# A convolution-attention kernel: the queues of all five engines ordered by a table of places, and the softmax's divisors kept in PSUM

## The chip, the cores and the metric

The kernel runs on one core of one Trainium2 chip. The metric is the device time of one execution in microseconds (us), and less is better. The core has a matrix engine (TensorE, in the profile PE, with its weight loads shown apart as PEld), a vector engine (VectorE, DVE), a scalar engine (ScalarE, ACT), a general one (GpSimd, POOL) and SyncE (SP), which here only issues DMAs. Each of the five works through a queue of its own, in order, and waits for the others by semaphores.

## The reference, cut to what matters

The input is 16 images of 56 x 56 pixels with 384 channels. Layer 0 is a group norm, then attention over a 3 x 3 neighbourhood with three dilations (one for each third of the channels, four heads of 32 channels in each), then a projection, added to the input. Layer 1 is a group norm and a depthwise 3 x 3 convolution with signs as weights, added again.

```python
def _dilate_attention(q, k, v, head_dim, kernel, dil):
    ...
    attn = jnp.einsum('bgdn,bgdkn->bgnk', qg, ku) * scale     # 9 neighbours
    attn = jax.nn.softmax(attn, axis=-1)
    out = jnp.einsum('bgnk,bgdkn->bgnd', attn, vu)
...
qkv = jnp.einsum('bchw,oc->bohw', xc, w_qkv)
outs = [_dilate_attention(qkv[:, 0, i], qkv[:, 1, i], qkv[:, 2, i], hd, 3, (1, 2, 3)[i]) for i in range(3)]
y = jnp.stack(outs, axis=3).reshape(b, h, w, c)
return jnp.einsum('bhwc,oc->bhwo', y, w_proj) + b_proj
...
x = x + _L0_conv_ref(_gn(x), w_qkv, w_proj, b_proj)
x = x + _L1_conv_ref(_gn(x), w)                               # depthwise, weights sign(clip(w))
```

## The kernel before

An image is cut into 7 chunks of 8 rows (448 pixels), so there are 112 chunks. Data lie with the channels on the partitions, 128 channels to a group, three groups. Everything is float32 but the attention weights, which are split into three bfloat16 terms. All loops are unrolled in Python, and three plans lay out a chunk's work:

- `plan_a`: a chunk of x is loaded, transposed on PE (`turn`, tile `pt_x`), copied out by ACT (`xa`), its statistics taken by DVE, and stored channel by channel.
- `plan_b`, attention. `normalise` (ACT, tile `xn`); `k_or_v` (PE, tile `pkv`, then a copy on ACT and two small DMAs for the rows shared with the next chunk) and `query` (PE, tile `pq`) for each of three groups. `score`, nine times: DVE multiplies a query by three shifted keys (`t`). `score_rounds`: PE sums these over a head's channels in bursts (`ps`, from 32-column pieces of the array). The softmax in five pieces: a copy `sT` on ACT, its transposes `pt_s` on PE, maximum and difference on DVE, `exp` on ACT, sum, reciprocal and product on DVE (L556 to L558, the divisors `sm` in SBUF), a cast on ACT and three operations on POOL that make the three terms; then a transposing DMA. `weigh`, nine times: PE spreads three weights over a head's channels (`pb_a`, three bfloat16 matmuls of 24 rows), DVE multiplies them by shifted values (`w`, L600), and POOL adds (L608, L611, L612) until `y` is there. `out_project`, three times: PE (`po`), then DVE adds the residual and takes statistics, and the sum is stored.
- `plan_c`, convolution: for two channel groups PE takes the side taps (`pc`, 32-column pieces), ACT normalises their input (`z`) and makes a term `u`, DVE adds three operands. For the third group ACT makes nine products (`taps_g`, L818) and POOL adds them (L825 to L834). Then everything is transposed back (`turn`, tile `pt_o`), copied out by ACT and stored.
- `group_norm`, once for each image and layer, turns statistics into a scale and a shift, in six pieces over PE, DVE and POOL.

A stage is one chunk in the steady part: the tile `sT` is written once in each. A stage is nine slices (`STEP`). Every piece is put down with `at(slice, order, piece)`: the slice is counted from the chunk's own start `t0`, and the second number orders the pieces within one slice (SOFTMAX first, LOADS last). At the end all pieces are traced in that order. The framework's scheduler then makes the five queues out of what was traced; it goes by priority in the order of tracing, by its own estimate of when operands are ready, and by when a buffer comes free. So an engine's queue may differ from the traced order, and a group of matmuls may be divided. `in_one_go` gives the later matmuls of a group a high priority and keeps them in order. Chunk m's attention starts at slice 9m; its stage A runs up to 12 stages ahead, its convolution ten stages behind.

Buffers that matter below: PSUM has 8 banks: three for everything that is short (`ps_mt`: `pt_x`, `pkv`, `po`, `pt_s`, `pc`, `pt_o` and the norm's tiles), one for `pq`, one for `ps`, three for one `pb_a`. In SBUF there are four `t`, four `w`, two `z`, two `x1`, two `xg`, two `xa`, one `u`, one `xin`, one `xr`.

Of the kernel before, what the change touches and what calls it, by code (L numbers as in the profile page):

```python
# [31 lines left out]
TERMS = 3  # L32


@with_exitstack
def dilated_attention_then_binary_conv(
# [263 lines left out]
    def in_one_go(matmuls):  # L300

        matmuls[0]()
        with tc.high_priority():
            for m in matmuls[1:]:
                tc.keep_in_program_order(m())

    def group_norm(sets):

        had = {}
        L = len(sets)

        def channels(n, j):
            if "ch" not in had:
                had["ch"] = st_p.tile([P, L, NG, 2], F32, tag=f"ch{L}", name="ch")
            nc.vector.bn_aggr(had["ch"][:, n, j, :], sets[n][0][:, j].rearrange("p c s -> p (c s)"))  # L320

        def mean():
            had["pair"] = pair = st_p.tile([GN_G, L, 3], F32, tag=f"pair{L}", name="pair")
            pm = ps_mt.tile([P, 512], F32, tag="mt", name="pm")
            for j in range(NG):
                nc.tensor.matmul(
                    pm[:GN_G, 0:L], gsel[:, j], had["ch"][:, :, j, 0], start=(j == 0), stop=(j == NG - 1)
                )
            nc.vector.tensor_scalar_mul(pair[:, :, 2], pm[:GN_G, 0:L], -1.0 / GN_CH)

        def deviation():

            ch = had["ch"]
            pb = ps_mt.tile([P, 512], F32, tag="mt", name="pb")
            for j in range(NG):
                nc.tensor.matmul(
                    pb[:, j * L : (j + 1) * L], gselT[:, j], had["pair"][:, :, 2], start=True, stop=True
                )
            had["dev"] = dev = st_p.tile([P, L, NG], F32, tag=f"dev{L}", name="dev")
            nc.vector.tensor_tensor(  # L340
                dev, pb[:, : NG * L].rearrange("p (j l) -> p l j", l=L), ch[:, :, :, 0], ALU.add
            )
            nc.gpsimd.tensor_tensor(dev, dev, dev, ALU.mult)
            nc.gpsimd.tensor_tensor(dev, dev, ch[:, :, :, 1], ALU.add)

        def variance():
            dev = had["dev"]
            pv = ps_mt.tile([P, 512], F32, tag="mt", name="pv")
            for j in range(NG):
                nc.tensor.matmul(pv[:GN_G, 0:L], gsel[:, j], dev[:, :, j], start=(j == 0), stop=(j == NG - 1))  # L350
            had["var"] = var = st_p.tile([GN_G, 3, L], F32, tag=f"var{L}", name="var")
            v, r = var[:, 0], var[:, 1]
            nc.vector.tensor_scalar(v, pv[:GN_G, 0:L], 1.0 / GN_CH, 1e-5, op0=ALU.mult, op1=ALU.add)

            ri = r.bitcast(I32)
            nc.vector.tensor_single_scalar(ri, v.bitcast(I32), 1, op=ALU.arith_shift_right)
            nc.vector.tensor_scalar(ri, ri, -1, RSQRT_BITS, op0=ALU.mult, op1=ALU.add)

        def invert():

            var, pair = had["var"], had["pair"]
            v, r, t = var[:, 0], var[:, 1], var[:, 2]
            for step in range(3):
                nc.gpsimd.tensor_tensor(t, r, r, ALU.mult)
                nc.gpsimd.tensor_tensor(t, t, v, ALU.mult)
                nc.gpsimd.tensor_scalar(t, t, -0.5, 1.5, op0=ALU.mult, op1=ALU.add)
                nc.gpsimd.tensor_tensor(pair[:, :, 1] if step == 2 else r, r, t, ALU.mult)
            nc.gpsimd.tensor_tensor(pair[:, :, 0], pair[:, :, 2], pair[:, :, 1], ALU.mult)

        def spread_out():  # L370
            pair = had["pair"]
            pp = ps_mt.tile([P, 512], F32, tag="mt", name="pp")
            for j in range(NG):
                nc.tensor.matmul(
                    pp[:, 2 * L * j : 2 * L * (j + 1)], gselT[:, j], pair[:, :, 0:2], start=True, stop=True
                )
            mr = st_p.tile([P, NG, L, 2], F32, tag=f"mr{L}", name="mr", bufs=5 - L)
            nc.vector.tensor_copy(mr.rearrange("p j l s -> p (j l s)"), pp[:, : 2 * L * NG])
            for n, (_, done, for_convolution) in enumerate(sets):
                if not for_convolution:  # L380
                    done(mr[:, :, n])
                    continue

                pz = ps_mt.tile([P, 512], F32, tag="mt", name="pz")
                for s in range(JG * NQ):
                    of_set = gselT[:, s // NQ, s % NQ * HD : s % NQ * HD + HD]
                    for ky in range(3):
                        nc.tensor.matmul(
                            pz[ky * HD : (ky + 1) * HD, 2 * s : 2 * s + 2], of_set, pair[:, n, 0:2],
                            start=True, stop=True,  # L390
                        )
                mrz = st_p.tile([K3, JG, NQ, 2], F32, tag="mrz", name="mrz")
                nc.vector.tensor_copy(mrz.rearrange("p j q s -> p (j q s)"), pz[:K3, : 2 * JG * NQ])
                done(mr[:, :, n], mrz)

        return channels, mean, deviation, variance, invert, spread_out
# [4 lines left out]
    pieces = {}  # L401

    def at(when, order, piece):

        pieces.setdefault((when, order), []).append(piece)
# [8 lines left out]
    def plan_a(m, t0):  # L414
# [17 lines left out]
        def turn(j):  # L432
# [5 lines left out]
            if b == 0:  # L438

                if j == 0:  # L440
                    pool, tag = ((xn_p, "xn"), (xn_p, "xn"), (xn_p, "xn"), (xr_p, "xr"), (t_p, "t"), (w_p, "w"),
                                 (w_p, "w"))[c]
                    first[c] = pool.tile([P, NG, PX], F32, tag=tag, name="x_first")
                xa = first[c][:, j]
            else:
                xa = xa_p.tile([P, PX], F32, tag="xa", name="xa")
            nc.scalar.copy(xa, pt[:, :PX])  # L447
            nc.vector.bn_stats(stats0[b][:, j, c, :], xa)
            if b:
                nc.sync.dma_start(xd[b][j * P : (j + 1) * P, c * PX : (c + 1) * PX], xa)  # L450
            elif j == NG - 1:
                nc.scalar.dma_start(chunk_of(xd[b], c), first[c])

        at(t0 - 3 if b else FIRST + 2 * max(c - 2, 0), LOADS, load)
        for j in range(NG):
            at(t0 + 2 * j if b else FIRST + 2 * c + 1, STAGE_A, lambda j=j: turn(j))

    def plan_b(m, t0):
# [21 lines left out]
        def k_or_v(g, which):  # L480
# [4 lines left out]
            project(pk, (1 + which) * C + g * P)  # L485
            nc.scalar.copy(cur[:, d : d + ROWS, d : d + W], rows(pk[:, :PX]))  # L486
            if c == 0:
# [7 lines left out]
        def query(g):  # L495
            had["q"] = pq = ps_q.tile([P, 512], F32, tag="q", name="pq")
            project(pq, g * P)
# [23 lines left out]
        def score(i):  # L521

            g, ky = divmod(i, 3)
            d = DIL[g]
            qg = rows(had["q"][:, :PX])
# [15 lines left out]
        def softmax_1():  # L541

            sT = s_p.tile([P, NSUB * NPAD * HEADS], F32, tag="sT", name="sT")[:, :PX]
            nc.scalar.copy(sT, had.pop("ps")[:, :PX])
            pt = ps_mt.tile([P, 512], F32, tag="mt", name="pt_s")
            for s in range(NSUB):
                nc.tensor.transpose(pt[:SUB, s * P : (s + 1) * P], sT[:, s * SUB : (s + 1) * SUB], permf)
            pt4 = pt[:SUB].rearrange("p (s v) -> p s v", s=NSUB)[:, :, :NR]
            mx = s_p.tile([SUB, NSUB, GH], F32, tag="mx", name="mx")
            nc.vector.reduce_max(mx, by_neighbour(pt4).rearrange("p s o k -> p s k o"), axis=AX.X)  # L550
            nc.vector.tensor_tensor(by_neighbour(weights), by_neighbour(pt4), over_neighbours(mx), ALU.subtract)
            nc.scalar.activation(weights, weights, AF.Exp, scale=SCALE)

        def softmax_2():
            sm = s_p.tile([SUB, NSUB, GH], F32, tag="mx", name="sm")
            nc.vector.reduce_sum(sm, by_neighbour(weights).rearrange("p s o k -> p s k o"), axis=AX.X)  # L556
            nc.vector.reciprocal(sm, sm)
            nc.vector.tensor_tensor(by_neighbour(weights), by_neighbour(weights), over_neighbours(sm), ALU.mult)  # L558

        EIGHTS = "p (u k) -> p u k"  # L560
        e8 = ew.rearrange(EIGHTS, k=8)
        term = [e3.rearrange("p s u (r k) -> p (s u r) k", r=4)[:, :, 8 * t : 8 * t + 8] for t in range(TERMS)]

        def softmax_3():

            nc.scalar.copy(term[0], e8)  # L566

        def softmax_4():
            had["rest"] = rest = s_p.tile([P, NSUB * NPAD * HEADS], F32, tag="sT", name="rest")[:SUB]
            nc.gpsimd.tensor_tensor(rest.rearrange(EIGHTS, k=8), e8, term[0], ALU.subtract)  # L570

        def softmax_5():
            r8 = had["rest"].rearrange(EIGHTS, k=8)
            nc.gpsimd.tensor_copy(term[1], r8)
            last_term[m] = nc.gpsimd.tensor_tensor(term[2], r8, term[1], ALU.subtract)

# [392 lines left out]
```

## Time and profile before

| what | value |
|---|---|
| time of three runs | 5153.74 us median (5148.28 to 5155.06) |
| the profiled execution's own time | 5160.07 us |
| its span, first to last instruction | 5157.9 us |
| mean granted PE clock | 0.979 |
| POOL `w<-w` (L608) | 672 of 3050 ns |
| DVE `w<-pb_a,v` (L600) / `t<-pq,k` (L529) | 1008 of 1549 ns / 1008 of 1547 ns |
| ACT `z` (L721) / `m<-zg,ktap` (L818) | 840 of 752 ns / 945 of 659 ns |
| DVE `ew<-ew,sm` (L558) | 112 of 1055 ns |
| loads `x<-x1d` / `z<-x1d` / `xin` | 5.7 / 3.8 / 7.8 us from issue to landing |

The profile is of one execution of its own. Busy shares are means over the whole span, and a busy PE is not PE at its peak, since its matmuls overlap; the distance from one matmul's start to the next is the better measure. float32 matmuls are two instructions each in the trace, so `pkv x12` is two projections and `pq x6` is one.

### The profile page before, as it was taken

What the parts mean: (1) busy time and instruction counts of PE and PEld (TensorE: products, weight loads), DVE (VectorE), ACT (ScalarE), POOL (GpSimd) and SP (SyncE); (2) the same over time, 40 slices, a digit from 0 to 9 for tenths busy, and PEclk for the clock granted to TensorE, in tenths of its full rate; (3) what the DMA queues carried; (4) which work ended last, traced back from release to release, by engine and by line L of the source; (5) the groups of instructions that cost most, each with busy time, mean ns of one, the idle gap of its engine ahead of it and who ended that gap; (6) DMA issues with size and microseconds to landing.
All of it is one profiled execution on the core that took longest, in us unless ns stands there. A gap on an engine that the chain in (4) does not pass through costs nothing. (4 is left out here: it accounts for less than half of the span.)

```text
span 5157.9 us, 72661 instructions
## 1 busy us (share of the span) xinstructions
PE 4967.5 (96%) x25093; PEld 2259.1 (44%) x25093; DVE 4475.9 (87%) x4575; ACT 2478.8 (48%) x4365; POOL 4248.0 (82%) x2998
## 2 busy tenths in 40 slices
PE   7999999999999999999999999999999999999975
PEld 4444444444444444444444444444444444444422
DVE  4888888888898888898888898888889988888876
ACT  3223545555454555545545554554555545444445
POOL 2778888888888888889888888888889888888891
PEclk8999999999999999999999999999999999999986
DMA  6443666666566665666666666666656656555455
GB/s 194 125 123 112 171 170 175 171 168 172 166 172 167 169 169 167 172 163 172 170 175 169 168 174 169 168 168 167 173 164 174 168 166 170 146 135 139 119 144 162
DMA packets 813957, 836.45 MB, mean 162 GB/s; under 512 B 362643, under 2 KB 782870, under 8 KB 813590
## 3 DMA queue, kind: packets, MB, share of 16 engines
q1 hardware_dynamic: 805606, 819.81, 57.8%
q10 hardware_dynamic: 7984, 12.00, 0.7%
q8 instruction: 199, 3.26, 0.3%
q14 instruction: 168, 1.38, 0.1%
HBM read 477.43 MB, written 231.21 MB: 137 GB/s over the span
## 5 line engine op out<-in xcount | busy, mean ns | idle before, releaser
L608 POOL TENSOR_TENSOR w<-w 128x1344 f32<-128x1344 f32 x672 | 2049.5, 3050 | 300.8 <-DVE w L600 262.3
L600 DVE TENSOR_TENSOR w<-pb_a,v 128x1344 f32<-128x1344 f32 x1008 | 1561.6, 1549 | 132.5 <-PE pb_a L593 102.1
L529 DVE TENSOR_TENSOR t<-pq,k 128x1344 f32<-128x1344 f32 x1008 | 1527.6, 1547 | 130.0 <-PE pq L476 128.8
L476 PE MATMUL pkv<-xn,wqkvT 128*128 128x448 f32 x3924 | 1553.3, 545 | 26.7 <-ACT xa L447 26.2
L476 PEld LDWEIGHTS pkv<-xn,wqkvT 128*128 128x128 f32 x3924 | 727.6, 191 | 706.4 <-issue 631.6
L476 PE MATMUL pq<-xn,wqkvT 128*128 128x448 f32 x1962 | 862.4, 567 | 0.0
L626 PE MATMUL po<-y,wprojT 128*128 128x448 f32 x2016 | 836.2, 551 | 20.1 <-POOL y L612 17.3
L721 ACT ACTIVATE z<-z,mrz 96x448 f32<-96x448 f32 x840 | 580.4, 752 | 262.6 <-DMA z<-x1d 220.6
L825 POOL TENSOR_TENSOR m<-m 128x1344 f32<-128x1344 f32 x210 | 640.0, 3047 | 68.6 <-ACT m L818 62.6
L514 PE MATMUL ps<-t,sel 128*32 128x448 f32 x6048 | 661.1, 546 | 1.8 <-DVE t L529 1.7
L818 ACT ACTIVATE m<-zg,ktap 128x448 f32<-128x448 f32 x945 | 568.9, 659 | 17.6 <-POOL m L825 8.5
L626 PEld LDWEIGHTS po<-y,wprojT 128*128 128x128 f32 x2016 | 375.8, 191 | 378.8 <-issue 346.2
L486 ACT COPY v<-pkv 128x448 f32<-128x448 f32 x336 | 178.5, 531 | 755.2 <-PE pkv L476 755.1
L476 PEld LDWEIGHTS pq<-xn,wqkvT 128*128 128x128 f32 x1962 | 339.4, 190 | 349.9 <-issue 349.9
L593 PE MATMUL pb_a<-aT,spread 24*128 24x448 bf16 x3024 | 370.4, 360 | 52.6 <-DVE w L600 48.4
L629 DVE SCALAR_TENSOR_TENSOR xr<-po,bias,xr 128x448 f32<-128x448 f32 x336 | 227.5, 677 | 210.7 <-PE po L626 205.8
L612 POOL TENSOR_TENSOR y<-y,w 128x448 f32<-128x448 f32 x336 | 381.7, 1136 | 20.3
L611 POOL TENSOR_TENSOR y<-w 128x448 f32<-128x448 f32 x336 | 382.3, 1138 | 17.3
L447 ACT COPY xa<-pt_x 128x448 f32<-128x448 f32 x315 | 167.4, 533 | 474.6 <-PE pt_x L435 469.2
L593 PEld LDWEIGHTS <-spread 24*128 24x128 bf16 x3024 | 102.5, 91 | 627.5 <-issue 608.6
L570 POOL TENSOR_TENSOR rest<-ew,e 112x512 f32<-112x512 f32 x112 | 130.2, 1163 | 292.5 <-ACT e L566 291.3
L752 PE MATMUL pc<-z,kdiag 96*32 96x440 f32 x3360 | 359.5, 546 | 8.8 <-POOL z L723 7.6
(141 smaller groups left out, 4745.8 us busy)
## 6 DMA issues: line engine op xcount, KB each, us to landing
z<-x1d SPq DMA_DIRECT2D x570, 224.0 KB, 3.8
xr<-xd SPq DMA_DIRECT2D x112, 672.0 KB, 4.3
x1d<-xr SPq DMA_DIRECT2D x112, 672.0 KB, 3.2
xn<-xd SPq DMA_DIRECT2D x109, 672.0 KB, 4.6
xin<-in_x_dram SPq DMA_DIRECT2D x105, 672.0 KB, 7.8
xd<-xa SPq DMA_DIRECT2D x315, 224.0 KB, 3.6
out_dram<-osb SPq DMA_DIRECT2D x420, 168.0 KB, 3.5
x<-x1d SPq DMA_DIRECT2D x80, 560.0 KB, 5.7
```

The lines of the kernel that those rows point to most:

```text
L476: nc.tensor.matmul(dst[:, :PX], wqkvT[:, cc, o0 : o0 + P], had["xn"][:, cc, :], start=(cc == 0), stop=(cc == NG - 1))
L514: return nc.tensor.matmul(had["ps"][32 * j : 32 * j + 32, :PX], sel[:, s0 : s0 + 32], tk, start=(issued[j] == 1), stop=(issued[j] == len(r ...
L529: nc.vector.tensor_tensor(t.rearrange("p k (r w) -> p k r w", w=W), q3, k3, ALU.mult)
L593: return nc.tensor.matmul(pb[:, kx, :PX].rearrange("p (s n) -> p s n", s=NSUB), spread[rows_of, v % 2, :], had["a"][rows_of, :, v // 8, :] ...
L600: nc.vector.tensor_tensor(w.rearrange("p k (r w) -> p k r w", w=W), pb[:, :, :PX].rearrange("p k (r w) -> p k r w", w=W), three(kv[1][g][m ...
L608: nc.gpsimd.tensor_tensor(w0, w0, w, ALU.add)
L611: nc.gpsimd.tensor_tensor(y, w0[:, 0], w0[:, 1], ALU.add)
L612: nc.gpsimd.tensor_tensor(y, y, w0[:, 2], ALU.add)
L626: nc.tensor.matmul(po[:, :PX], wprojT[:, g, j * P : (j + 1) * P], had[f"y{g}"], start=(g == 0), stop=(g == NG - 1))
L721: nc.scalar.activation(z, z, AF.Identity, bias=mrz[:, j, q, 0:1], scale=mrz[:, j, q, 1:2])
L818: nc.scalar.activation(rows(t[:, kx]), zp[:, ky : ky + ROWS, kx : kx + W], AF.Copy, scale=ktap[:, JG, o : o + 1])
L825: nc.gpsimd.tensor_tensor(had["m"], had["m"], t, ALU.add)
```

## The change

Three things change. The tables of slices go, and a table `WHEN` takes their place: it holds, for each kind of work and each of its repetitions, one number for every engine's part of it, in slices from t0. The pieces become generators that `yield` between the parts of different engines, and `put` places each part by its own number. While the place lies from 0 to 9 x 112 + 14 = 1022, every instruction of the five queues is tied to the one traced before it on its engine (`pin`), so that each queue has exactly the traced order; outside that stretch the scheduler orders as before. And the divisors `sm` are written to a PSUM tile in the bank of `ps`, not to SBUF.

```diff
+WHEN = dict(
+    load_in=[[1.86]],
+    turn_in=[[6.026, 7.853, 8.103, 9.616], [8.887, 8.898, 11.431, 13.527], [9.427, 9.669, 9.841, 12.978]],
+    load_x=[[-16.698]],
+    normalise=[[-14.8], [-11.887], [-14.8]],
+    k=[[-7.795, -7.784, -7.773], [-6.349, -6.338, -2.8], [-3.845, -3.158, -1.177]],
+    v=[[7.341, 7.352, 8.827], [5.08, 6.207, 9.429], [7.847, 8.378, 9.967]],
+    query=[[4.619], [7.271], [8.939]],
+    score=[[4.825], [5.138], [5.149], [7.626], [7.637], [7.877], [10.723], [10.734], [10.745]],
+    burst=[[5.75], [8.056], [11.108]],
+    softmax=[[11.283, 12.017, 12.028, 12.151, 13.101, 13.445, 14.191, 14.202, 14.629, 15.664]],
+    weigh=[[17.248, 17.838, 20.379], [18.267, 18.278, 20.39], [20.023, 20.034, 20.421], [20.194, 20.223,
+        23.104], [20.709, 20.932, 24.835], [21.886, 22.889, 25.743], [23.429, 23.44, 25.754], [23.902, 25.371,
+        27.079], [25.884, 25.895, 27.807]],
+    load_residual=[[28.002]],
+    out_project=[[28.362, 28.749, 29.829, 108.842], [28.647, 29.405, 34.465, 55.401], [30.355, 30.533, 31.612,
+        34.476]],
+    load_g=[[9.822]],
+    normalise_g=[[10.839]],
+    taps=[[11.121, 12.433], [11.132, 12.731], [11.143, 14.144]],
+    sums=[[18.53], [18.541], [18.813]],
+    load_x1=[[5.837]],
+    load_z=[[-1.661, 3.083], [1.74, 3.075]],
+    normalise_z=[[5.379, 5.39], [7.123, 7.821]],
+    column=[[6.427], [7.222]],
+    convolve=[[5.632, 6.438], [8.054, 8.065]],
+    turn_out=[[19.405, 19.416, 19.866], [20.439, 20.499, 20.51], [21.786, 21.835, 27.008], [22.192, 22.518,
+        22.582]],
+    statistics=[[33.116, 34.74, 35.945, 35.956, 37.004, 37.015, 37.026, 37.993, 38.004, 39.539, 40.578, 40.589,
+        40.926, 40.937, 41.368]],
+)
...
-        with tc.high_priority():
+        with nullcontext() if newest.get("pinned") else tc.high_priority():
             for m in matmuls[1:]:
-                tc.keep_in_program_order(m())
+                if newest.get("pinned"):
+                    m()
+                else:
+                    tc.keep_in_program_order(m())
...
+    def put(t0, what, piece):
+
+        places = WHEN[what]
+        for n, stages in enumerate(places):
+            of_it = (n,) if len(places) > 1 else ()
+            if len(stages) == 1:
+                at(t0 + stages[0], lambda of_it=of_it: piece(*of_it))
+                continue
+            steps = piece(*of_it)
+            for when in stages:
+                at(t0 + when, lambda steps=steps: next(steps, None))
...
-            sm = s_p.tile([SUB, NSUB, GH], F32, tag="mx", name="sm")
+            yield
+            sm = ps_s.tile([P, 512], F32, tag="s", name="psm")[:SUB, : NSUB * GH]
+            sm = sm.rearrange("p (s k) -> p s k", s=NSUB)
             nc.vector.reduce_sum(sm, by_neighbour(weights).rearrange("p s o k -> p s k o"), axis=AX.X)
             nc.vector.reciprocal(sm, sm)
+            yield
             nc.vector.tensor_tensor(by_neighbour(weights), by_neighbour(weights), over_neighbours(sm), ALU.mult)
...
-        at(t0 - 18, LOADS, load_x)
...
-        at(t0 + 9, SOFTMAX, softmax_1)
-        at(t0 + 10, SOFTMAX, softmax_2)
...
-            at(t0 + 14 + i - (pair == 1), WEIGH_AHEAD if pair == 0 else WEIGH, lambda i=i: weigh(i))
-        at(t0 + 20, LOADS, load_residual)
-        for j in range(NG):
-            at(t0 + 24 + j, PROJECT, lambda j=j: out_project(j))
+        put(t0, "load_x", load_x)
...
+        put(t0, "softmax", softmax)
+        put(t0, "weigh", weigh)
...
+            t0 += max(0, WHEN["statistics"][0][-1] + 1.1 - 36)
...
-            ahead = 8 if c else 1
+            ahead = 8 if c > 1 else 1
...
+    def pin(engines):
+
+        traced = nc.cur_bb.bb.instructions
+        new = []
+        for ins in reversed(traced):
+            if ins is newest.get("seen"):
+                break
+            new.append(ins)
+        newest["seen"] = traced[-1]
+        for ins in reversed(new):
+            if ins.engine not in FIXED:
+                continue
+            prev = newest.get(ins.engine)
+            newest[ins.engine] = ins
+            if prev is not None and ins.engine in engines:
+                tc.add_manual_dep(
+                    ins, prev.name,
+                    mybir.DependencyInfo(mybir.DependencyClass.NoSync, mybir.DependencyReason.DATA),
+                    reason="stage order",
+                )
+
+    for when in sorted(pieces):
+        newest["pinned"] = FROM <= when < UNTIL
+        for piece in pieces[when]:
             piece()
+            pin(FIXED if newest["pinned"] else ())
```

The numbers of one list are the parts of one piece in order: for a softmax ACT, PE, DVE, ACT, DVE (sum and reciprocal), DVE (product), ACT, POOL, POOL, SP; for `weigh` PE, DVE, POOL; for `out_project` PE, DVE, DVE, SP; for `turn_in` PE, ACT, DVE, SP; for `k` and `v` PE, ACT, SP; for `convolve` PE, DVE; for `turn_out` PE, ACT, SP; for `statistics` DVE, DVE, PE, DVE, PE, DVE, POOL, PE, DVE, POOL, PE, DVE, PE, DVE, POOL. A last number that meets a generator already at its end does nothing. `group_norm` is one generator now, with the same operations; `softmax_1` to `softmax_5` and `turn_weights` are one too. Assertions at the time of tracing check that a reused buffer holds what its reader expects. The first image's stage A, the last image's convolution and the chunks up to number 14 of stage A keep whole pieces at one place; the last image's convolution is moved 6.47 slices later in the order of tracing. No operation is added or taken away, and none changes its engine.

## The prediction

> **What bounds the kernel now.** I read the page first (busy shares, the slices), then the softmax copies by tile, which tick once per stage, then a table of windows for five single stages, and then one stage on PE's timeline.
>
> ```profile
> PE 4967.5 (96%) x25093; PEld 2259.1 (44%) x25093; DVE 4475.9 (87%) x4575; ACT 2478.8 (48%) x4365; POOL 4248.0 (82%) x2998
> ...
> PEclk8999999999999999999999999999999999999986
> ```
> ```profile
> L544 ACT COPY sT<-ps x89: 506/533/537, 506.3 to 4378.1; 128x448 f32<-128x448 f32 x89
> ...
> L544 ACT COPY sT<-ps x14: 506/522/533, 4378.1 to 4967.0; 128x448 f32<-128x448 f32 x14
> ```
> ```profile
> 2177.60:2221.00 43.40, 43.11 (x216) 19.42 (x213) 38.48 (x38) 23.00 (x41) 37.40 (x23) 1.00 0.61 165
> 2264.30:2311.30 47.00, 45.56 (x288) 22.11 (x285) 42.63 (x48) 15.99 (x30) 38.26 (x40) 1.00 0.60 164
> 2311.30:2355.40 44.10, 44.09 (x218) 19.71 (x216) 38.86 (x39) 28.03 (x53) 39.37 (x24) 1.00 0.61 173
> 4558.90:4605.40 46.50, 44.86 (x204) 19.39 (x201) 38.53 (x35) 21.69 (x37) 37.78 (x24) 0.93 0.48 129
> ```
> The columns of the windows are length, then busy PE, PEld, DVE, ACT, POOL. The copies give 3871.8/88 = 44.0 us a stage up to 4378 and 588.9/13 = 45.3 after it. A plain stage is 43.4, the one with a group norm 47.0, the next 44.1: an image is 308. The late stage has no stage A and yet is longer.
>
> ```profile
> 2180.00 2.42 PE L626 MATMUL po<-y,wprojT 128*128 128x448 f32 x6
> 2182.25 0.60 PE L547 MATMUL pt_s<-perm,sT 128*112 128x128 f32 x4
> 2182.69 4.67 PE L476 MATMUL pkv<-xn,wqkvT 128*128 128x448 f32 x12
> 2187.20 0.55 PE L435 MATMUL pt_x<-ident,xin 112*128 112x112 f32 x4
> ...
> 2192.20 2.52 PE L476 MATMUL pq<-xn,wqkvT 128*128 128x448 f32 x6
> 2194.65 0.36 PE L593 MATMUL pb_a<-aT,spread 24*128 24x448 bf16 x3
> ...
> 2195.61 0.27 PE L841 MATMUL pt_o<-ident,xg 128*112 128x128 f32 x1
> 2196.17 4.78 PE L476 MATMUL pkv<-xn,wqkvT 128*128 128x448 f32 x12 [0.29 <-ACT xa L447]
> 2200.78 0.38 PE L841 MATMUL pt_o<-ident,x 128*112 128x128 f32 x2
> ```
> By starts, 12 projections' halves take 4.51 us (2182.69 to 2187.20), 0.376 each[...], and the clock is full. So a plain stage is a full PE queue. What is left in it: `pq` between two `pb_a` takes 2.45, `po` after a `pq` and ahead of `pt_s` 2.25. I read 0.1 us for entering, and 0.1 for leaving, a run of full-array work (`pkv`, `pq`, `po`, transposes) from the array's pieces (`pb_a`, `ps`, `pc`). And one wait, for the PSUM buffer that ACT's copy `xa` frees: from 2195.61 to 2200.78 is 5.17 where such rows take 0.11 + 4.51 elsewhere, 0.55 lost.
>
> The divisors, in the view of L558 and late in the timeline:
>
> ```profile
> L558 DVE TENSOR_TENSOR ew<-ew,sm x112: 586/608/3077, 109.9 to 4975.1; 112x432 f32<-112x432 f32 x112
> ...
> 4569.55 2.04 DVE L558 TENSOR_TENSOR ew<-ew,sm 112x432 f32<-112x432 f32 x1
> ...
> 4573.11 0.37 PE L593 MATMUL pb_a<-aT,spread 24*128 24x448 bf16 x3 [1.64 <-DVE w L600]
> ```
> The median is 608 ns, the longest about a POOL `w<-w` (3050): the product waits behind POOL. Late on, a `w` queued behind it then holds up PE.
>
> [...]
>
> **The change, part by part.**
> *PE's order.* Places modulo 9 give the new stage (square brackets: full-array runs): [pt_x2 k0 po0 pt_o0 po1] pb2 burst2 pb3 [pt_o1 k1] pb4 [pt_s po2 pt_o2] pb5 [pt_o3 q0 v1 k2] pb6 pc0 burst0 pb7 [pt_x0 q1 v0 v2] pb8 pc1 burst1 pb0 [pt_x1 q2] pb1. That is 6 runs; the timeline of before has 8 (two single `pt_o` or `pq` runs and a divided `pq` among them). Two runs less at 0.2: -0.4. The `xa` wait: after pt_x0 at least q1 (2.25) stands ahead of the next buffer taken: -0.55. Everything else is the same work. 43.40 - 0.95 = 42.45 us.
>
> *Do the others keep up?* I set the groups end to end from pt_x2 = 0.3 (`k`, `v`, `q`, `po` 2.25, three `pb_a` 0.3, `pc` 1.6, bursts 1.64 and 2.39, transposes 0.4). DVE by starts: `w` and `t` 1.47 each, 18 of them 26.4; `xr` 3 x 0.6; statistics 6 x 0.53; `pc`'s operations 2.4 + 1.1; softmax 3.0 with L558 at 0.53: 37.9 of 42.45. POOL 37.4 (the window). DVE's tight places: w8, pc1's three operations and w0 end at 41.7, and pb1 needs the bank at 42.4; t2 ends at 26.4 for burst0 at 26.8; maximum and difference end at 16.8 and free a bank for pt_o3 at 17.6. ACT: nine taps in one row (9 x 0.66) end at 13.0, sT at 13.5, pt_s is due at 14.2; z0 ends at 24.2, pc0 is due at 25.2. POOL: y0 comes at about 1.5 of the next stage, po0 is due at 3. SP has v0's DMAs issued at 34.4, w0 starts at 41; load_x1 waits behind pt_o3's store (20.5) and lands at 26.3 by its 5.7 us, where ACT wants `u` at 26.7. The two row DMAs of `k` and `v` stand 2 to 4 slices behind their copies on SP, yet each is issued before its reader by 3 us or more; osb2's store, put at 27.0, goes out at 34.4 and lands by 38 (3.5 us), before the next pt_o0 takes that buffer at 6. In an image's first and last chunk POOL's edge memset stands ahead of the casts and waits for z0: 1.6 of POOL's 4.8 us of slack. The ties add no semaphore; what they cost is that nothing passes a late instruction any more. All margins hold, most by 0.4 to 1 us. For what slips I allow 0.2 a stage (bounds 0 and 1.0).
>
> *Divisors.* Two SBUF inputs become one: at most 0.61, saving the mean's 0.45 a stage on DVE; hidden behind PE in plain stages, part of the late gain below. The bank is idle between sT (11.3) and the next burst0 (14.75), and the product's place is 13.4: no new wait. Sum and reciprocal now write PSUM, which no row here shows; L550 reads PSUM in 596 ns and L551 in 589, so I take 0, bounds -0.3 and +0.3, under DVE's slack.
>
> *Group norm.* The stage and its next cost 4.3 more now. PE's own part, by starts, is 2.5; three new run changes 0.6; L356, 2.63 us behind POOL in most, falls where POOL waits for w2 behind it, so near 0.2; POOL's thirteen small operations (2.5 us) end about when their matmul is due: 0.4. Sum 3.5.
>
> *Sum.* Image: 7 x 42.65 + 3.5 = 302.0 against 308.1: -6.1, times 88/7: -77. Late 13 stages: 42.45 less three pt_x (1.3) plus 0.4 (POOL at 91%), twice the norm, stage A in two: 13 x 41.55 + 7 + 2.6 = 550 against 589: -39. First ten stages (405.3): no convolution, 0.8 each: -8. Fill before: the same chain, 0. Tail: weighing lies later, at sT of the last chunk POOL has the whole previous chunk's adds left (25 us; now about 17), and 1.2 chunks of convolution more, beside idle engines: +15 (bounds 0 and +35). Together -109: 5160.07 - 109 = 5051 for an execution like the profiled, which stood 6.3 above the median: 5045.
>
> **The rivals.**
> *Stalls move (B).* Fixed order gains nothing on PE, because what the order saves comes back as waits at the tight places: stages stay 43.4. Image 307.3: -9; late stages 1.0 above A's, 562: -27; tail +15: 5160 - 21 - 6 = 5133. For: six margins under 1 us. Against: DVE has 4.5 us of slack to recover in.
> *Slower (C): ACT's row of taps ahead of sT.* A fixed PE queue can't pass pt_s. ACT waited 168.0 us in 84 times for xg's load (2.0 each, longest 8.6). If zg starts late, all nine taps do, then sT, then pt_s. The margin is 0.7; from 1.6 late the gain is gone; 3.0 late gives 44.95 a stage with the allowance: image 318, +125; late part 579, -10; tail +15: 5284. Against: load_g stands at 0.82 on SP behind DMAs that are ready at 35, some 13 us ahead of zg.
> *It doesn't do what it says (D):* the ties bind nothing new, only the divisors act. Late stages lose their L558 waits, about 2 us each: 5153.7 - 26 = 5128.
>
> **Numbers.** A measurement of this kernel can tell about 0.2% from no change (10 us). Chances: A (my forecast) 0.63, B 0.18, C 0.15, D 0.04. Likeliest 5045. A's own range: no slips (-18), tail 0 (-15), run changes 0.2 a stage better (-20) give 4990; slips of 1.0 (+80) and the tail's 20 give 5145. With B and D inside and some room for the fill, 4975 to 5150, C left out. Faster: nearly all of A, two thirds of B, D: 0.78; same 0.05; slower 0.17.
>
> **What would show it.** Plain stages of 42.3 to 42.8 and no PE wait for `xa`; L558 never over 0.7; norm stages together +3 to +4; late stages near 41.5; sT to the last `y` longer by 5 to 10. Wrong if PE waits for sT or DVE by a microsecond in each stage, or if the tail grows by over 35.

## The result, and the profile after

The changed kernel takes 5093.29 us (median of 4 runs, 5086.65 to 5096.50) beside 5152.51 for the kernel before: a ratio of 0.9884, 95% interval 0.9867 to 0.9901. The profiled execution took 5091.71 us, its span is 5089.7. Forecast were 5045 and a range of 4975 to 5150: faster, as said, and inside the range, but with 59 us gained where 109 were worked out. The range held with room that was meant for other terms: the largest miss, in the first ten stages, had no term of its own in it.

First the page of the changed kernel, then its softmax copies by tile in three stretches (first ten stages, the 88 steady ones, the late 13), then the windows of a plain stage, of two norm stages in neighbouring images, and of the stage ahead of the second (the column behind POOL's is the granted clock).

```profile
PE 4883.7 (96%) x25093; PEld 2242.3 (44%) x25093; DVE 4434.3 (87%) x4575; ACT 2476.1 (49%) x4365; POOL 4253.3 (84%) x2998
...
PEclk8999999999999999999999999999999999999976
```
```profile
L613 ACT COPY sT<-ps x11: 532/533/533, 110.7 to 536.7; 128x448 f32<-128x448 f32 x11
...
L613 ACT COPY sT<-ps x89: 504/508/532, 536.7 to 4329.8; 128x448 f32<-128x448 f32 x89
...
L613 ACT COPY sT<-ps x14: 504/509/513, 4329.8 to 4877.9; 128x448 f32<-128x448 f32 x14
```
```profile
2432.90:2475.10 42.20, 42.20 (x214) 19.25 (x213) 38.85 (x39) 22.30 (x40) 38.02 (x26) 1.00 0.60 160
2301.80:2348.40 46.60, 44.32 (x269) 20.62 (x268) 39.30 (x41) 22.62 (x43) 41.35 (x42) 1.00 0.59 160
2603.00:2651.30 48.30, 46.02 (x269) 21.09 (x268) 39.35 (x41) 22.68 (x43) 41.34 (x42) 0.96 0.57 155
2559.40:2603.00 43.60, 43.48 (x232) 20.50 (x231) 40.04 (x50) 22.85 (x43) 38.52 (x28) 1.00 0.64 173
```

The page alone says nothing: PE is 96% busy before and after. The copies say where the time went. In the spans of the two profiled executions:

| stretch | before | after | difference | forecast |
|---|---|---|---|---|
| up to the first copy | 101.0 | 110.7 | +9.7 | 0 |
| first ten stages | 405.3 | 426.0 | +20.7 | -8 |
| 88 steady stages | 3871.8 | 3793.1 | -78.7 | -77 |
| late 13 stages | 588.9 | 548.1 | -40.8 | -39 |
| last copy to the end | 190.9 | 211.8 | +20.9 | +15 |

Together the spans differ by 68 us where 109 were forecast. The two gains came in the forecast size (the steady one in part by luck, as shown below), and the beginning, which was forecast to gain 8, lost 30. A plain stage has gone from 43.4 to 42.2 us, but a norm stage takes 46.7 or 48.3, mostly in turn, and the one ahead of it 43.5. Counted over a whole plain stage, PE has 6 runs of full-array work where it had 8. PE's timeline of the changed kernel, in a plain stage:

```profile
2438.41 2.42 PE L528 MATMUL pq<-xn,wqkvT 128*128 128x448 f32 x6
2440.67 4.67 PE L528 MATMUL pkv<-xn,wqkvT 128*128 128x448 f32 x12
2445.27 0.36 PE L660 MATMUL pb_a<-aT,spread 24*128 24x448 bf16 x3
2445.57 1.68 PE L818 MATMUL pc<-z,kdiag 96*32 96x440 f32 x16
2447.07 1.69 PE L574 MATMUL ps<-t,sel 128*32 128x448 f32 x16
2448.69 0.36 PE L660 MATMUL pb_a<-aT,spread 24*128 24x448 bf16 x3
2448.99 0.60 PE L476 MATMUL pt_x<-ident,xin 112*128 112x112 f32 x4
2449.42 2.43 PE L528 MATMUL pq<-xn,wqkvT 128*128 128x448 f32 x6
2451.70 4.67 PE L528 MATMUL pkv<-xn,wqkvT 128*128 128x448 f32 x12
```
One sees the run `q0 v1 k2` go through at 2.26 and 4.60 by starts, with the 0.1 only where `pb_a` follows, and no wait. `pc` right ahead of `ps` takes 1.50 from start to start. The kernel before, in a plain stage:

```profile
2188.78 1.71 PE L514 MATMUL ps<-t,sel 128*32 128x448 f32 x16
2190.30 1.66 PE L752 MATMUL pc<-z,kdiag 96*32 96x440 f32 x16
2191.90 0.36 PE L593 MATMUL pb_a<-aT,spread 24*128 24x448 bf16 x3
...
2203.97 1.68 PE L752 MATMUL pc<-z,kdiag 96*32 96x440 f32 x16
2205.59 1.02 PE L476 MATMUL pq<-xn,wqkvT 128*128 128x448 f32 x2
```
There a `pc` took 1.60 ahead of a `pb_a` and 1.62 ahead of a `pq`, and one `ps` right ahead of a `pc` took 1.52.

### The profile page after: what moved, and what is told of

Its sections match the earlier page's. It is cut to its first block, busy times and chain, and to the rows that moved or that the text cites. A ratio compares the mean times of both kernels' runs of the same rounds, so it can differ in the third digit from the quotient of the medians.

```text
span 5089.7 us, 72426 instructions
## 1 busy us (share of the span) xinstructions
PE 4883.7 (96%) x25093; PEld 2242.3 (44%) x25093; DVE 4434.3 (87%) x4575; ACT 2476.1 (49%) x4365; POOL 4253.3 (84%) x2998
## 4 chain that ended last, share of the span: by engine, by line
PE 78%; DVE 6%; POOL 5%; issue 2%; ACT 2%; DMA 2%; SPq 0%; ACTq 0%; DVEq 0%; POOLq 0%
PE pkv L528 24%; PE po L699 13%; PE pq L528 13%; PE ps L574 10%; PE pc L818 6%; PE pb_a L660 5%; PE pt_o L909 3%; PE pt_x L476 3%; DVE w L671 3%; POOL w L681 2%; DVE t L593 2%; PE pt_s L617 1%; ACT z L786 1%; POOL m L892 1%; DMA z<-x1d 1%
## 5 line engine op out<-in xcount | busy, mean ns | idle before, releaser
L699 PE MATMUL po<-y,wprojT 128*128 128x448 f32 x2016 | 824.6, 546 | 18.6 <-POOL y L685 18.0
L528 PE MATMUL pq<-xn,wqkvT 128*128 128x448 f32 x1962 | 811.4, 550 | 0.0
L574 PE MATMUL ps<-t,sel 128*32 128x448 f32 x6048 | 664.7, 549 | 36.6 <-DVE t L593 36.4
L786 ACT ACTIVATE z<-z,mrz 96x448 f32<-96x448 f32 x840 | 570.2, 751 | 101.8 <-DVE mrz L414 97.1
L882 ACT ACTIVATE m<-zg,ktap 128x448 f32<-128x448 f32 x945 | 540.4, 655 | 9.8 <-ACT zg L860 0.4
L528 PEld LDWEIGHTS pq<-xn,wqkvT 128*128 128x128 f32 x1962 | 350.3, 192 | 253.8 <-issue 253.5
L541 ACT COPY k<-pkv 128x448 f32<-128x448 f32 x336 | 180.1, 536 | 547.2 <-PE pkv L528 547.2
L684 POOL TENSOR_TENSOR y<-w 128x448 f32<-128x448 f32 x336 | 381.3, 1135 | 26.2
L574 PEld LDWEIGHTS ps<-t,sel 128*32 128x32 f32 x6048 | 190.4, 110 | 390.6 <-issue 293.4
```

What stands on the lines that cost most here:

```text
L528: nc.tensor.matmul(dst[:, :PX], wqkvT[:, cc, o0 : o0 + P], had["xn"][:, cc, :], start=(cc == 0), stop=(cc == NG - 1))
L574: return nc.tensor.matmul(had["ps"][32 * j : 32 * j + 32, :PX], sel[:, s0 : s0 + 32], tk, start=(issued[j] == 1), stop=(issued[j] == len(r ...
L699: nc.tensor.matmul(po[:, :PX], wprojT[:, g, j * P : (j + 1) * P], had[f"y{g}"], start=(g == 0), stop=(g == NG - 1))
L786: nc.scalar.activation(z, z, AF.Identity, bias=mrz[:, j, q, 0:1], scale=mrz[:, j, q, 1:2])
L882: nc.scalar.activation(rows(t[:, kx]), zp[:, ky : ky + ROWS, kx : kx + W], AF.Copy, scale=ktap[:, JG, o : o + 1])
```

## The experiments

Twelve kernels were run, each beside the kernel before on its chip, which took 5148.72 to 5152.54 us there; so differences between two rows hold to about 4 us. The last columns are from the starts of the softmax copies: the median of the 88 steady stages, and their mean.

| run | us | ratio (95% interval) | plain | mean |
|---|---|---|---|---|
| e1, before with divisors in PSUM | 5124.27 | 0.9951 (0.9937 to 0.9964) | 43.5 | 43.97 |
| e2, divisors back in SBUF | 5282.58 | 1.0253 (1.0239 to 1.0267) | 44.4 | 45.02 |
| e3, ties from slice 90 | 5058.27 | 0.9817 (0.9804 to 0.9830) | 42.2 | 43.19 |
| e4, inverse root earlier | 5048.30 | 0.9799 (0.9786 to 0.9813) | 42.2 | 42.79 |
| e5, one run more on PE | 5126.17 | 0.9956 (0.9942 to 0.9970) | 42.4 | 43.52 |
| e6, ties on PE | 5347.65 | 1.0388 (1.0373 to 1.0404) | 44.4 | 45.80 |
| e7, no ties | 5342.17 | 1.0372 (1.0352 to 1.0392) | 44.1 | 45.56 |
| e8, e3 and e4 | 5012.64 | 0.9736 (0.9722 to 0.9749) | 42.2 | 42.78 |
| e9, ties on PE, POOL | 5568.49 | 1.0808 (1.0790 to 1.0826) | 47.2 | 48.17 |
| e10, ties on PE, DVE, POOL | 5489.72 | 1.0659 (1.0644 to 1.0675) | 45.3 | 47.10 |
| e11, e8 with the end untied | 5023.16 | 0.9752 (0.9738 to 0.9767) | 42.2 | 42.78 |
| e12, ties on all but SP | 5099.90 | 0.9903 (0.9887 to 0.9920) | 42.2 | 43.18 |

### e1 and e2: the divisors alone, and the order without them

e1 puts three lines of the change into the kernel before; e2 takes them out of the changed one.

```diff
-            sm = s_p.tile([SUB, NSUB, GH], F32, tag="mx", name="sm")
+            sm = ps_s.tile([P, 512], F32, tag="s", name="psm")[:SUB, : NSUB * GH]
+            sm = sm.rearrange("p (s k) -> p s k", s=NSUB)
```


> The kernel before with only the divisors in PSUM; no order changed. If the divisors act by themselves (the product L558 then never waits for POOL): the product is 0.6 us always, the 13 late stages lose about 2 us each, the plain stages stay 43.4 (PE's queue is full there): about 26 us less than before, ratio 0.995. Rival, the divisors only matter within the new order: 5 us or less, ratio 0.999 to 1.001, the late stages at 45.

Measured: 26 us less, as the first theory said. In the profiled executions the late 13 stages fall from 588.9 to 556.7 us and the plain ones stay; these two executions lie further apart (42 us) than the medians. Two views by line, of e1 and then of e2, and e2's timeline where the product stands:

```profile
L559 DVE TENSOR_TENSOR ew<-ew,psm x112: 577/604/606, 109.7 to 4940.9; 112x432 f32<-112x432 f32 x112
```


> The changed kernel with the divisors back in SBUF. The product stands on DVE at a place where POOL runs a 3 us sum in most stages. If the order has slack enough on DVE (about 4 us a stage): product mean 1.5 to 2.5 us, plain stages 42.2 to 42.4, the time within 15 us of the changed kernel, ratio to before 0.988 to 0.992. Rival, the order needs the divisors in PSUM because nothing can pass the blocked product: 1 us or more of PE waiting in each stage, plain stages 43.2 or more, 100 us more than the changed kernel, ratio 1.005 or more.

```profile
L631 DVE TENSOR_TENSOR ew<-ew,sm x112: 607/3162/3566, 114.8 to 5075.1; 112x432 f32<-112x432 f32 x112
```
```profile
2519.66 6.15 POOL L891 TENSOR_TENSOR m<-m 128x1344 f32<-128x1344 f32 x2
2523.09 3.18 DVE L631 TENSOR_TENSOR ew<-ew,sm 112x432 f32<-112x432 f32 x1
2526.73 1.53 DVE L593 TENSOR_TENSOR t<-pq,k 128x1344 f32<-128x1344 f32 x1
...
2529.78 0.36 PE L659 MATMUL pb_a<-aT,spread 24*128 24x448 bf16 x3 [0.99 <-DVE w L670]
...
2532.71 1.71 PE L574 MATMUL ps<-t,sel 128*32 128x448 f32 x16 [0.95 <-DVE t L593]
```
Measured: 189 us more than the changed kernel; the rival was right. In the order of the table the product meets POOL's sums of taps in most stages (median 3162 ns), everything behind it on DVE is late by 2.5 us, PE waits first for `w` (0.99) and then for `t` (0.95), and the plain stage is 2.2 us longer. DVE is idle for over 3 us of each stage, yet that did not help: the bursts' margin there was 0.4. The order can't do without this small edit. Alone the edit is worth 26 us, and the order adds 31 to it (5124.27 to 5093.29).

### e5: the price of a run on PE

```diff
-    weigh=[[17.248, 17.838, 20.379], [18.267, 18.278, 20.39], [20.023, 20.034, 20.421], ...
+    weigh=[[17.248, 17.838, 20.379], [18.267, 18.278, 20.39], [19.45, 20.034, 20.421], ...
```


> The changed kernel with PE's part of one weighing (the third, pb2) moved from 20.023 to 19.45, that is from behind po1 to between pt_o0 and po1; its vector operation and everything else keep their places. PE now has 7 runs of full-array work in a stage, not 6. If entering and leaving a run cost 0.2 us together, as the prediction read it: plain stages 42.4 (42.2 in the changed kernel), about 20 us more than the changed kernel, ratio to before 0.991 to 0.994. Rival, the 0.2 us are an artefact of the starts, hidden behind the stream: plain stages 42.2, the time within 6 us of the changed kernel, 0.987 to 0.990.

Measured: plain stages of 42.39 us beside 42.20, so 0.19 for one run more. PE's timeline of e5 around the moved weighing:

```profile
2442.85 0.27 PE L909 MATMUL pt_o<-ident,xg 128*112 128x128 f32 x1
2443.06 0.36 PE L660 MATMUL pb_a<-aT,spread 24*128 24x448 bf16 x3
2443.35 2.52 PE L699 MATMUL po<-y,wprojT 128*128 128x448 f32 x6
2445.80 2.46 PE L574 MATMUL ps<-t,sel 128*32 128x448 f32 x22
```
The transpose ahead of `pb_a` now takes 0.21 to the next start (0.11 in the changed kernel, where `po` follows), and `po` 2.45 (2.35). The whole run costs 33 us, not 20: the norm stages also grew, to 48.8 and 50.1 in two neighbouring images:

```profile
1095.20:1144.00 48.80, 46.11 (x269) 21.42 (x268) 39.16 (x41) 22.69 (x43) 42.85 (x42) 0.97 0.60 153
1399.70:1449.80 50.10, 47.62 (x269) 22.26 (x268) 39.18 (x41) 22.72 (x43) 42.86 (x42) 0.93 0.56 149
```
Most of the rest is the clock. In the steady part of e5 the granted clock was halved for 54.6 us in all, in the changed kernel for 17.1; work at half speed in the other 37.5 us costs about 19 (an estimate), and 88 stages at 0.19 cost 17. Together that is about the 36.6 us by which the steady part grew.

### e3, e4 and e8: the beginning and the norm

```diff
-    FROM, UNTIL = 0, STEP * N + 14
+    FROM, UNTIL = 10 * STEP, STEP * N + 14
```


> The changed kernel with the ties only from slice 90 on; all places stay. If the ties cost the first stages their time (the order is made for stages with a convolution, and without its matmuls pb_a and the bursts stand too close behind the vector engine): the first ten stages fall from 426 to about 405 us, all else as in the changed kernel: 20 to 30 us less, ratio to before 0.982 to 0.985. Rival, the places themselves cost it (later stage A and values in the order of tracing): the first ten stages stay at 420 or more, the time within 8 us of the changed kernel.

Measured: 35 us less than the changed kernel. The first ten stages take 398.2 us, less than before's 405.3, and the first copy comes at 99.6, with the same places. So the ties cost the beginning its time. PE's waits for `t` in the first ten stages, in the changed kernel (110 to 537 us) and then in e3 (99 to 498):

```profile
PE ps L574 <- DVE t L593: 25.6, 13, 5.4
...
PE ps L574 <- DVE t L593: 2.9, 2, 1.8
```
What the ties do is seen in the changed kernel's timeline of the sixth stage:

```profile
336.34 0.36 PE L660 MATMUL pb_a<-aT,spread 24*128 24x448 bf16 x3
338.61 3.09 PE L574 MATMUL ps<-t,sel 128*32 128x448 f32 x16 [1.91 <-DVE t L593]
```
No `pc` stands between them yet, so the burst is due 1.6 us sooner, and its margin is 0.4; behind it the matmuls run at the half clock (3.09 for a burst of 1.69; the granted clock from 338.6 to 341.7 is 0.53).

```diff
-        37.004, 37.015, 37.026, 37.993, 38.004, 39.539, 40.578, ...
+        37.004, 37.015, 37.026, 37.993, 38.004, 38.405, 40.578, ...
```


> The changed kernel with one place moved: POOL's thirteen small operations of the norm (the inverse root) from 39.539 to 38.405, ahead of a POOL sum that waits for DVE. If PE's wait for them is what makes the norm stage dear: no PE wait for pair any more, the norm stage 46.7 to 48.3 falls to 45 to 45.6 in every image and the half-speed clock windows once in two images go: 30 to 45 us less than the changed kernel, ratio to before 0.980 to 0.983. Rival, the wait only moves to the POOL sum behind them (y later, then po): norm stages fall by under 0.5, ratio 0.987 to 0.990.

Measured: 45 us less; the norm stages of the steady part take 45.0 to 45.3, and the clock is full all through it. The changed kernel's timeline shows the wait that went, the waits of e4 what is left of it in the whole execution (in the changed kernel that line reads 30.9 us in 17 times):

```profile
2610.36 0.18 POOL L391 TENSOR_TENSOR pair<-pair 32x2 f32<-32x2 f32 x1
2610.60 0.74 PEld L396 LDWEIGHTS pp<-pair,gselT 32*128 32x128 f32 x6 [1.81 <-POOL pair L391]
2610.60 0.83 PE L396 MATMUL pp<-pair,gselT 32*128 32x4 f32 x6 [1.57 <-POOL pair L391]
```
```profile
PE pp L396 <- POOL pair L391: 4.0, 1, 4.0
```
The thirteen operations of 0.18 us follow each other at 0.27, so they take 3.4 us and not 2.5; at their first place they came after the sums of `y`. At 38.405 they fill POOL's wait for `w` (3.82 us in that norm stage of the changed kernel).

> The ties from slice 90 on and POOL's inverse root at 38.405 together. If the two losses are separate, they add: 35 and 45 us less than the changed kernel, 5010 to 5020 us, ratio to before 0.972 to 0.975. Rival, the scheduler's first ten stages disturb the phase of what follows or the gains overlap: 5030 or more, ratio 0.977 or more.

Measured: 5012.64 us, 81 less than the changed kernel where 35 and 45 add to 80. The two losses are separate, and this kernel beats both.

### e6, e7, e9, e10, e12: which ties

Each changes one line, the engines whose queues are tied (e7: `FROM, UNTIL = 0, 0`).

```diff
-FIXED_ENGINES = ("PE", "DVE", "Activation", "Pool", "SP")
+FIXED_ENGINES = ("PE",)
```


> The changed kernel with ties on PE's queue alone; DVE, ACT, POOL and SP are ordered by the scheduler from the same places. If all queues must be held, since PE can't pass a late operand and the margins are under 1 us (the divisors' run showed it): plain stages 43.4 or more, ratio to before 1.0 or more. Rival, PE's own order carries the gain and the others have slack: plain stages 42.2 to 42.6, ratio 0.985 to 0.993.

> The changed kernel with no ties at all: the places only set the order of tracing, and the scheduler makes all five queues, as before. If the ties are what makes the queues: PE has again 7 or 8 runs a stage and waits, plain stages 43 or more, ratio 0.995 or more. Rival, the order of tracing alone does it (in_one_go's priority included): plain stages 42.2 to 42.5, ratio 0.985 to 0.990.

> Ties on PE and POOL only. With ties on PE alone, PE waited for POOL's y ahead of a projection. If POOL's order is what was missing: no PE wait for y, plain stages 42.2 to 42.8, ratio to before 0.987 to 0.997. Rival, DVE's order counts as well, since POOL waits for DVE's products in the scheduler's order: plain stages 43.3 or more, ratio 1.0 or more.

> Ties on PE, DVE and POOL; ACT and SP are ordered by the scheduler. If the three busy engines' order is enough, with ACT at half its time and SP only issuing: plain stages 42.2 to 42.5, ratio 0.986 to 0.992. Rival, ACT's row of taps and copies must be placed too (margin 0.7 us ahead of the softmax's transposes): plain stages 42.8 or more, ratio 0.997 or more.

> Ties on PE, DVE, ACT and POOL; SP's DMA issues alone are ordered by the scheduler. With ACT free too, PE waited for ACT's copy xa and the stage was 45 to 49. If ACT's queue was what was missing there: plain stages 42.2 to 42.5, ratio to before 0.985 to 0.992. Rival, SP's order was it (a store or a load queued ahead of what a stage needs): plain stages 43.3 or more, ratio 1.0 or more.

Measured: with no ties, or with PE's alone, the places are worse than the old slices (5342 and 5348). What PE waits for is POOL. In most plain stages PE's order is the table's, group for group, in e6 and also in e7, which ties nothing: 6 runs and no wait for `xa`. PE's timeline of e7:

```profile
2137.84 1.67 PE L699 MATMUL po<-y,wprojT 128*128 128x448 f32 x4
2141.00 1.02 PE L699 MATMUL po<-y,wprojT 128*128 128x448 f32 x2 [1.49 <-POOL y L685]
```
So there the order of tracing alone gives PE its queue, and what the ties add is in the queues that feed it. Tying POOL as well, and then POOL and DVE, with ACT free, is worse still (5568, 5490). The waits of e6, then of e10 (us in total, times, longest):

```profile
PE po L699 <- POOL y L685: 174.9, 86, 9.3
```
```profile
DVE stats L491 <- ACT xa L489: 380.2, 91, 7.6
...
PE po L699 <- ACT xa L489: 123.5, 77, 3.3
```
In e10 the copy `xa` is late in ACT's free queue, PE stops for the PSUM buffer that it frees, and DVE's tied queue stops at the statistics of `xa`, with all its products behind. ACT is 49% busy and still had to be placed: with it (e12) the plain stage is 42.2 again. SP's ties are not told apart from nothing (e12's interval overlaps the changed kernel's). Ties on DVE, ACT or POOL were not taken away one at a time, so which of the three could be spared stays open. The times that I expected for e6 and e7 held, but not e7's 7 or 8 runs: its plain stages have 6, like the changed kernel's. For e9 and e10 the rivals held, for e12 the first theory.

### e11: the end

```diff
-    FROM, UNTIL = 10 * STEP, STEP * N + 14
+    FROM, UNTIL = 10 * STEP, STEP * (N - 1)
```


> The kernel with ties from slice 90 and the early inverse root, and the ties ended at slice 999, one stage and a half sooner (1022 before). If the ties cost the end its time (POOL has the previous chunk's sums ahead of it at the last sT): from the last sT to the last y 74.6 falls to about 68, the last stages rise by 1 to 2: 3 to 8 us less than without it. Rival, the places alone make the end longer: the same within 4 us, or some us more since the scheduler's order is worse in the last stages.

Measured: 10.5 us more than e8. From the last copy to the last `y` 69.5 us instead of 74.6, but the last two stages 52.3 and 44.8 instead of 40.5 and 40.0. The scheduler gains 5 us on the way to the last `y` and pays 16 ahead of it. More than half of the end's loss is in the places: with no ties at all (e7) last copy to end is still 203, 12 more than before, of the changed kernel's 21.

## Why the prediction was right, and where its sum was off

- *PE is full in a plain stage, and runs cost 0.2.* Right. The stage fell by 1.2, forecast 0.75 with the allowance. e5 measured 0.19 for a run. The waits for `xa` went (26.2 us on PE in 78 times before, none listed on PE after). Mis-sized: the floor, 42.45 for 42.20. By starts, the groups in pieces of the array (`pb_a`, `ps`, `pc`) take 11.30 us of a plain stage where they took 11.46, which was forecast to stay: `pc` stands ahead of `ps` twice, and before there was one such pair. The full-array groups fell by 1.02 for 0.95. Mis-sized too is the allowance of 0.2 for slips, which came to 0: the tight margins held in plain stages.
- *Divisors hidden in plain stages, part of the late gain.* Right in time (e1: 26 us, D's forecast was 26; the late stages 40.8 for 39, of which e1 has 32 with the order unchanged). But "the order needs them" was not said: e2 shows that without them the change is 2.5% slower than before. That the product would be at most 0.61 was an estimate; before has one operation of the same shape with a PSUM input, L551 (`ew<-pt_s,mx`), at 585/589/608 ns in all 112, beside 586/608/3077 for the product. Measured: 577/604/606 in e1, 603/603/605 in the changed kernel. Sum and reciprocal in PSUM cost nothing to speak of: 935 and 466 ns, 911 and 453 before.
- *Norm stages, +3.5.* Too small: 5.8 and 7.5 in turn (46.7 + 43.5, and 48.3 + 43.6, less twice 42.2). The failed term is "end about when their matmul is due: 0.4". PE waited 1.57, because I took the operations' durations for their spacing, which the kernel before shows too (0.26 to 0.27); and in about every second image the wait fell so that the clock was halved in the next window (0.96 in the longer stage). e4 takes the wait away and has 45.0. The norm's integer shift (L383) is 156 ns, down from 2.63 us, as said. This error and the first one cancel in the steady sum, 7 times 0.45 against 2.3 to 4.0, so -78.7 for -77 is luck in part. The 44.1 of before was also misplaced: its window runs past the next copy, which starts at 2354.7. The stage right after the norm's is 43.4, and the one behind it 44.1; the image's 308 stays.
- *The beginning, -8 and 0.* Wrong, and the largest miss: +20.7 and +9.7, 38 of the 41 us between the spans' forecast and result. I took PE's work off (no convolution) and kept the margins. With PE's groups gone the vector engine's products come too late for the same order, and e3 shows that the ties do it.
- *The end, +15.* Nearly right: 20.9; the way to the last `y` grew by 11.3 (5 to 10 said), what comes after it by 9.6.
- *The rivals.* B's stalls did not come in plain stages; its mechanism is real, as e2 shows. C did not happen: PE never waited for `sT`, and ACT waited for xg's load once, for 1.5 us (84 times before). D is excluded by e7, whose queues without ties give 44.1 and 5342 us.

## What to carry to other kernels

When an engine is truly full, read its next starts, not its busy share: there the price of each change of tiling and each buffer wait can be read, and the sum of them is what an order can gain. A queue fixed by hand is only as good as its smallest margin to the engines that feed it; it fits one regime, so try another order for the beginning and for the end (here 35 us gained at the one, 10 lost at the other), and when queues are fixed, don't leave out a half-idle engine that computes (here ACT, 49% busy: 5489.72 us without ties on it and SP, 5099.90 with ACT's). Before fixing an order, remove what makes a duration vary with a neighbour, here the product that waited for POOL (607 to 3566 ns in e2, 603 to 605 in the changed kernel).

## What the hardware showed beyond expectation

- The norm's POOL operations of 0.18 us, each of which reads what the one before wrote, follow each other at 0.27 us with no wait in the profile. Spacing is not the same for all small operations: of two on 128 x 6 elements the second doesn't read the first's result, and it follows at 0.16, while of two others of that shape the second does (L370 and L371, 2593.90 and 2594.17), and it follows at 0.27. Whether the dependence makes the difference was not tested. The changed kernel's timeline:

```profile
2610.09 0.19 POOL L390 TENSOR_TENSOR pair<-var 32x2 f32<-32x2 f32 x1
2610.36 0.18 POOL L391 TENSOR_TENSOR pair<-pair 32x2 f32<-32x2 f32 x1
...
2617.70 0.20 POOL L728 TENSOR_TENSOR cs<-ktap,mr 128x6 f32<-128x6 f32 x1
2617.86 0.19 POOL L731 TENSOR_TENSOR cs<-kcol,mr 128x6 f32<-128x6 f32 x1
```
- A PE wait of 1.6 us can cost 3.3 (norm stages of 48.3, where e4 has 45.0). In five of the 12 norm stages of the steady part the granted clock was halved for one window of 3.41 us. Two windows at the wait with the half clock, and two in the image ahead of it, without:

```profile
2608.70:2612.10 3.40, 1.83 (x11) 1.31 (x10) 2.58 (x5) 2.57 (x5) 2.84 (x8) 1.00 0.15 44
2612.10:2615.50 3.40, 3.40 (x8) 1.05 (x8) 0.07 (x1) 0.00 (x0) 3.32 (x2) 0.50 0.70 195
2308.30:2311.70 3.40, 2.31 (x10) 1.61 (x11) 1.82 (x5) 1.75 (x4) 3.10 (x5) 1.00 0.36 72
2311.70:2315.10 3.40, 3.40 (x56) 1.83 (x55) 2.39 (x2) 0.00 (x0) 3.32 (x2) 1.00 0.51 171
```
  In all five the whole wait (1.57 us) fell into one window of the clock's record, and the next was halved; in the other seven it fell across two, with at most 1.24 us in either, and none was. In the clock's record of before and of the changed kernel every stretch of one clock, up to the last, is a whole multiple of 3.413 us. The five halved windows start at 1403.75, 2007.91, 2612.07, 3216.23 and 3820.39, which is 604.16 apart, or 177.0 windows; by the starts of the norm stages an image takes 301.2 us without the half clock and 302.9 with it, together 604.1. So after two images the wait stands at the same place in a window. In e5 three images take 914.9 us, 268.0 windows, and the norm stages there repeat mostly in threes (48.8, 48.8, 50.1). In the prediction's late stage (granted clock 0.93) the half clock from 4574.60 to 4581.43 follows a window with 1.64 us idle, which is all that PE was without work there (46.50 less 44.86). A fixed limit is not shown: before, from 4659.9 on, a window with 1.69 us idle is followed by a full clock.
- A burst of 32-column pieces ahead of another such burst takes 0.1 us less to the next start than ahead of `pb_a` or of full-array work: `pc` 1.50 against 1.60 and 1.62, by the timelines of the result's section.
